# A first stage written out as a table of ten steps, in one stream of recurrences with the layers

## Chip, core and metric

One Trainium2 chip, one NeuronCore. A core has five engines with queues of their own: PE (TensorE, matmuls; PEld are its weight loads), DVE (VectorE), ACT (ScalarE), POOL (GpSimd) and SP (SyncE, which here issues DMAs). Each takes its instructions in the order of its queue. They meet through semaphores. SBUF holds tiles of 128 partitions; PSUM, eight banks of 128 x 512 float32, takes the results of PE. The metric is the device time of one launch in microseconds (us), lower is better.

## What is computed

Two blocks on x of 4 sequences (b) x 1024 tokens x 128 features, all float32. First a two-directional state-space block, whose result is added to x:

```python
xn = _layernorm(x, ln_w, ln_b)
y_fwd = _mamba(xn, ...)
y_bwd = flip(_mamba(flip(xn), ...))
return x + 0.5 * (y_fwd + y_bwd)

def _mamba(x, ...):
    xp, z = split(x @ W_in.T)                      # 256 channels each
    xc = silu(conv4(xp) + b_conv)                  # depthwise, 4 taps
    dt, Bm, Cm = split(xc @ W_x.T, [8, 24])        # 8, 16, 16
    dt = softplus(dt @ W_dt.T + b_dt)
    A = -exp(A_log)
    def step(h, inp):                              # 256 channels x 16 states
        h = h * exp(dt_t[:, :, None] * A) + (dt_t * u_t)[:, :, None] * B_t[:, None, :]
        return h, einsum('bdn,bn->bd', h, C_t)
    y = (scan(step) + xc * Dp) * silu(z)
    return y @ W_out.T
```

Then six layers of windowed attention (16 heads of 64, window 32, rotary embedding, normalised queries and keys) and a gated feed-forward block of 341. They need, besides the weights, a rotary table for each layer (multiplied by the layer's scales) and first weights and biases into which the layer norm's scale and shift are folded.

## The kernel before

There are two parts. **`mamba` (L153)** is the first stage. The order in which its instructions reach the queues is left to the framework's scheduler. `prepare(b, d, out)` does for sequence b and direction d all that comes ahead of the recurrence: load and normalise (for d = 0), transpose, convolution as four accumulated matmuls, gate product, Silu, the small projection `xdbl`, softplus as five ACT steps (L320 to L324) and three DVE steps (L328 to L330), and stores to DRAM: `gate`, `xcs` (convolved input), `bcd` (B and C) and `dts` (dt, and dt times the input). There are eight such (b, d) units. `scan(d, ready, m, more)` runs the recurrence of sequence 0 alone, for one direction and one half m of the channels, on tiles of 32 channels x 4 states by 1024 tokens: 4 x 16 such tiles, that is 128 tiles' worth of 512 tokens. Time runs along the free axis, one `tensor_tensor_scan` for each 512 tokens. Between the tiles it pulls pieces of the generator `beside()` (L483): the preparation of the other units, and for every layer `rotary` and `fold`. What is left of them follows after the last scan, then the projection of direction 1 and `store(0)`, which hands sequence 0 to the layers in `xsa`.

**`Layers` (L803)** is the rest, in a fixed order. Its 96 tiles (sequence, layer, 256 tokens) go through the table `ORDER`, one pass per tile; an entry `name-back` is the operation `name` for the tile that lies `back` passes behind. Entries of `ASIDE` (xd, xi, xr, xo, xt, xa, xy, xg, xp, xq) are turns of **`Beside` (L504)**, which runs the recurrences of sequences 1 to 3 beside the layers. It cuts them into units (b, d, half of time t, half of channels m) of 16 scan tiles of 8 channels x 16 states by 512 tokens, 384 in all, 6 in each pass of ORDER: `fetch`/`steps` loads `sdt0` and `sdt1` three tiles ahead (three buffers each, 256 KB a load), `decay` (L631) makes exp(dt A) on ACT into `da`, which has one PSUM buffer, `input` (L643 on POOL for odd tiles, L645 on DVE for even ones) makes the input term in `sh` (eight buffers), `scan` (L659) is on DVE, `output` (L672) multiplies by C on POOL, `add` (L692) sums over the states on PE for four tiles, `skip` (L705), `gate` (L716), and `piece` p or q advances the output projection. When the stream is over, the passes go on with `LAST_ORDER`, which has no turns of Beside. At the seam, the constants are made a second time (`make_consts`, L61, with the attention masks), SP issues the first layer's weights (24 DMAs), then `beside.start()` its first loads. In the first pass 8 x FIRST (L1353), one turn of each kind, runs eight tiles at once.

Of the kernel before, what the change touches and what calls it, by code (L numbers as in the profile page):

```python
# [18 lines left out]
P = 128  # L19
# [40 lines left out]
@with_exitstack  # L60
def make_consts(ctx, tc, pool, first):  # L61

    nc = tc.nc
    c = {}
    c["ident"] = pool.tile([P, P], F32, name="ident")
    make_identity(nc, c["ident"])
    if first:
        flip = c["flip"] = pool.tile([P, P], F32, name="flip")
        nc.gpsimd.memset(flip, 0.0)
        nc.gpsimd.affine_select(  # L70
            out=flip, in_=flip, pattern=[[1, P]], compare_op=ALU.not_equal,
            fill=1.0, base=-(P - 1), channel_multiplier=1,
        )

        ones = pool.tile([P, DG], F32, name="ones")
        nc.gpsimd.memset(ones, 1.0)
        nc.gpsimd.affine_select(
            out=ones, in_=ones, pattern=[[-SG, DG]], compare_op=ALU.is_ge,
            fill=0.0, base=0, channel_multiplier=1,
        )  # L80
        states = c["states"] = pool.tile([P, DG], F32, name="states")
        nc.gpsimd.affine_select(
            out=states, in_=ones, pattern=[[SG, DG]], compare_op=ALU.is_ge,
            fill=0.0, base=SG - 1, channel_multiplier=-1,
        )
    else:
        flip = c["flip"] = pool.tile([P, P], F32, name="flip")
        nc.gpsimd.memset(flip, 0.0)
        nc.gpsimd.affine_select(
            out=flip, in_=flip, pattern=[[1, P]], compare_op=ALU.not_equal,  # L90
            fill=1.0, base=-(P - 1), channel_multiplier=1,
        )

        wide = c["states"] = pool.tile([P, 2 * DG - DG8], F32, name="wide")
        nc.gpsimd.memset(wide, 0.0)
        nc.vector.tensor_reduce(
            wide[:, DG - DG8 : DG], c["ident"].rearrange("p (n i) -> p i n", i=DG8),
            AX.X, ALU.add,
        )
        ident16 = c["ident16"] = pool.tile([P, P], BF16, name="ident16")  # L100
        nc.vector.tensor_copy(ident16, c["ident"])
        mean = c["mean"] = pool.tile([P, P], F32, name="mean")
        nc.vector.memset(mean, 1.0 / D)
        center = c["center"] = pool.tile([P, P], F32, name="center")
        nc.vector.tensor_tensor(center, c["ident"], mean, ALU.subtract)

        tp = ctx.enter_context(tc.tile_pool(name="t_mask", bufs=1))
        m32 = tp.tile([P, 8, 2 * W], F32, name="m32")
        nc.gpsimd.memset(m32, 0.0)
        for r in range(4):  # L110
            q = m32[r * W : (r + 1) * W]
            nc.gpsimd.affine_select(
                out=q, in_=q, pattern=[[0, 8], [1, 2 * W]], compare_op=ALU.is_ge,
                fill=NEG, base=0, channel_multiplier=-1,
            )
            nc.gpsimd.affine_select(
                out=q, in_=q, pattern=[[0, 8], [-1, 2 * W]], compare_op=ALU.is_ge,
                fill=NEG, base=W, channel_multiplier=1,
            )
        mask = c["mask"] = pool.tile([P, 8, 2 * W], BF16, name="mask")  # L120
        nc.vector.tensor_copy(mask, m32)

        mask0 = c["mask0"] = pool.tile([P, 8, 2 * W], BF16, name="mask0")
        nc.vector.tensor_copy(mask0, m32)
        nc.vector.memset(
            mask0[0:W].rearrange("p (h x) j -> p h x j", x=2)[:, :, 0, 0:W], NEG
        )
    return c
# [23 lines left out]
@with_exitstack  # L152
def mamba(  # L153
    ctx, tc, dram, x, lnwb, win, wconv, wx, wdt, wout, vecs, alog, x1_dram, xsa, spilled,
    rope, qks, tabs, w1, lvec, w1f, lvf
):
# [3 lines left out]
    nc = tc.nc  # L160
    nc.scalar.preload_act_table_set("natural_log_exp_and_others")
    cp = ctx.enter_context(tc.tile_pool(name="m_const", bufs=1))
    c = make_consts(tc, cp, True)
    ident, flip, states = c["ident"], c["flip"], c["states"]
    eps = cp.tile([P, 1], F32, name="m_eps")
    nc.vector.memset(eps, EPS)

    x_tiled = x.rearrange("(n p) d -> p n d", p=P)
    lnwb_sb = cp.tile([P, 2], F32, name="lnwb_sb")
    nc.scalar.dma_start(out=lnwb_sb, in_=lnwb)  # L170
    w = []
    for d in range(2):
        wd = {

            "wtap": cp.tile([P, KC, DI], F32, name=f"wtap{d}"),
            "wz": cp.tile([P, DI], F32, name=f"wz{d}"),
            "wx": cp.tile([P, NC, NX], F32, name=f"wx{d}"),
            "wdt": cp.tile([RANK, DI], F32, name=f"wdt{d}"),
            "wout": cp.tile([P, NC, D], F32, name=f"wout{d}"),
            "vec": cp.tile([P, NC, 3], F32, name=f"vec{d}"),  # L180
            "nega": cp.tile([P, NC, NDG, NSG], F32, name=f"nega{d}"),
        }
        nc.scalar.dma_start(
            out=wd["wtap"], in_=wconv[d : d + 1].to_broadcast([P, KC, DI])
        )
        nc.scalar.dma_start(out=wd["wz"], in_=win[d, :, 0:DI])
        nc.vector.tensor_tensor(
            wd["wtap"], wd["wtap"], bc(wd["wz"], 1, [P, KC, DI]), ALU.mult
        )
        nc.scalar.dma_start(out=wd["wz"], in_=win[d, :, DI:])  # L190
        nc.scalar.dma_start(out=wd["vec"], in_=vecs[d].rearrange("(c p) k -> p c k", p=P))
        nc.scalar.dma_start(out=wd["wx"], in_=wx[d].rearrange("(c p) k -> p c k", p=P))
        nc.scalar.dma_start(out=wd["wdt"], in_=wdt[d])
        nc.scalar.dma_start(out=wd["wout"], in_=wout[d].rearrange("(c p) k -> p c k", p=P))
        na = wd["nega"].rearrange("p m q g -> p (m q g)")
        nc.scalar.dma_start(out=na, in_=alog[d])
        nc.scalar.activation(na, na, AF.Exp)
        nc.vector.tensor_scalar(na, na, -1.0, None, ALU.mult)
        w.append(wd)

    sp = ctx.enter_context(tc.tile_pool(name="m_seq", bufs=1))
    wp = ctx.enter_context(tc.tile_pool(name="m_work", bufs=2))
    ps = ctx.enter_context(tc.tile_pool(name="m_ps", bufs=4, space=PSUM))
    psd = ctx.enter_context(tc.tile_pool(name="m_psd", bufs=2, space=PSUM))
    psy = ctx.enter_context(tc.tile_pool(name="m_psy", bufs=1, space=PSUM))

    def one(name):

        return ps.tile([P, TC], F32, name=name, tag="bank")

    seq = [None] * B

    def load(b):

        x1 = sp.tile([P, NBLK, D], F32, name="x1b" if b else "x1")
        xl = sp.tile([P, NBLK, D], F32, name="xl")
        s = slice(b * NBLK, (b + 1) * NBLK)
        nc.sync.dma_start(out=x1, in_=x_tiled[:, s, :])
        mv, rstd = norm_stats(nc, sp, x1, NBLK, eps, "x")
        normalize(nc, xl, x1, mv, rstd, NBLK)  # L220
        mv, rstd = norm_stats(nc, sp, xl, NBLK, eps, "l")
        nc.gpsimd.tensor_tensor(x1, x1, xl, ALU.add)
        normalize(nc, xl, xl, mv, rstd, NBLK)
        if b:
            nc.sync.dma_start(out=x1_dram[:, s, :], in_=x1)
        seq[b] = (x1, xl)

    def prepare(b, d, out):

        if d == 0:  # L230
            load(b)
        yield
        xl = seq[b][1]
        wd = w[d]
        vec = wd["vec"]
        halves = [slice(t * TC, (t + 1) * TC) for t in range(NTC)]

        xnT = sp.tile([P, KC - 1 + T], F32, name="xnT")
        nc.gpsimd.memset(xnT[:, 0 : KC - 1], 0.0)
        for t in range(NTC):  # L240
            pm = one("pm")
            for i in range(4):
                k = t * 4 + i
                s = slice(i * P, (i + 1) * P)
                if d == 0:
                    nc.tensor.transpose(pm[:, s], xl[:, k, :], ident)
                else:
                    nc.tensor.matmul(
                        pm[:, s], lhsT=xl[:, NBLK - 1 - k, :], rhs=flip, start=True, stop=True
                    )  # L250
            at = KC - 1 + t * TC
            nc.vector.tensor_scalar(
                xnT[:, at : at + TC], pm, lnwb_sb[:, 0:1], lnwb_sb[:, 1:2], ALU.mult, ALU.add
            )
            yield
# [92 lines left out]
    def spread(name, src):  # L348
# [5 lines left out]
        )  # L354
        return tile_

    def scan(d, ready, m, more):


        wd = w[d]  # L360
# [1115 lines left out]
```

## Time and profile before

| what | value |
|---|---|
| runs | 4144.86 us median of 3 (4140.26 to 4152.97) |
| profiled execution, own time | 4133.05 us |
| its span, first to last instruction | 4131.3 us |
| mean granted TensorE clock | 0.952 |
| busy in the span | PE 3794.3, DVE 3385.5, POOL 3214.1, ACT 2952.0 us |
| DMA | 518.28 MB, 125 GB/s in the mean |
| Gelu of the layers' first and last tile | 747.1 and 4119.7 us |

The layers' first matmuls run at 584, and their second pass begins at 640. The stretch with ORDER lasts to about 2950, that with LAST_ORDER to the end. In lines of groups, "x" is the number of instructions, then busy us, mean ns of one, idle time of the engine just before them, and after "<-" who ended most of it. Matmul ends are modelled, so a busy PE isn't PE at its peak.

### The profile page before, as it was taken

What the parts mean: (1) busy time and instruction counts of PE and PEld (TensorE: products, weight loads), DVE (VectorE), ACT (ScalarE), POOL (GpSimd) and SP (SyncE); (2) the same over time, 40 slices, a digit from 0 to 9 for tenths busy, and PEclk for the clock granted to TensorE, in tenths of its full rate; (3) what the DMA queues carried; (4) which work ended last, traced back from release to release, by engine and by line L of the source; (5) the groups of instructions that cost most, each with busy time, mean ns of one, the idle gap of its engine ahead of it and who ended that gap; (6) DMA issues with size and microseconds to landing.
All of it is one profiled execution on the core that took longest, in us unless ns stands there. A gap on an engine that the chain in (4) does not pass through costs nothing.

```text
span 4131.3 us, 144710 instructions
## 1 busy us (share of the span) xinstructions
PE 3794.3 (92%) x62120; PEld 2433.6 (59%) x62120; DVE 3385.5 (82%) x5053; ACT 2952.0 (71%) x5533; POOL 3214.1 (78%) x2463
## 2 busy tenths in 40 slices
PE   5666757999999999999999999999999999999998
PEld 2122223666666666666666666666666666666666
DVE  4665637999999899999999999999777777777774
ACT  4654634787778777878777877778667777777776
POOL 3779519999989898999889999989666666666663
PEclk8766767999999999999999999999999999999999
DMA  5654244555555555555454555554212222222221
GB/s 191 204 174 161 108 152 138 152 161 153 153 144 149 146 153 155 154 151 164 139 149 144 157 157 164 161 143 132 65 56 60 60 64 62 60 60 61 58 60 43
DMA packets 308111, 518.28 MB, mean 125 GB/s; under 512 B 43464, under 2 KB 135120, under 8 KB 307472
## 3 DMA queue, kind: packets, MB, share of 16 engines
q1 hardware_dynamic: 303136, 506.74, 41.6%
q8 instruction: 491, 8.04, 0.8%
q10 hardware_dynamic: 4336, 2.28, 0.2%
q14 instruction: 148, 1.21, 0.1%
HBM read 362.85 MB, written 48.52 MB: 100 GB/s over the span
## 4 chain that ended last, share of the span: by engine, by line
PE 65%; ACT 8%; DVE 5%; POOL 4%; issue 2%; DMA 1%; SPq 0%; DVEq 0%; ACTq 0%; POOLq 0%
PE pq L905 13%; PE po L1090 10%; PE pw L1112 8%; PE pv L957 7%; PE pt L988 6%; PE sim L1027 5%; PE pe L1065 4%; PE py L1209 3%; PE pa L1193 3%; PE pg L1169 2%; ACT sq L912 2%; PE sim L1009 2%; PE acc L692 1%; DVE rot L925 1%; DVE r L925 1%
## 5 line engine op out<-in xcount | busy, mean ns | idle before, releaser
L938 POOL TENSOR_TENSOR r<-r,rot 128x512 f32<-128x512 f32 x768 | 965.0, 1275 | 81.0 <-DVE rot L925 70.5
L951 POOL TENSOR_TENSOR r<-r,n 128x1024 f32<-128x1024 f32 x384 | 726.7, 1907 | 252.8 <-ACT n L947 242.0
L905 PE MATMUL pq<-w,xsa 128*128 128x512 f32 x1536 | 798.0, 614 | 13.7 <-DMA w<-in_wqkv 11.4
L925 DVE TENSOR_TENSOR rot<-pq,tab 128x512 f32<-128x512 f32 x768 | 516.2, 683 | 139.5 <-ACT sq L912 107.7
L912 ACT ACTIVATE sq<-pq 128x512 f32<-128x512 f32 x768 | 448.4, 599 | 242.7 <-PE pq L905 124.8
L925 DVE TENSOR_TENSOR r<-pq,tab 128x512 f32<-128x512 f32 x768 | 518.2, 683 | 72.0 <-ACT sq L912 39.9
L1058 POOL TENSOR_TENSOR e<-e,sm 128x1024 f32<-128x1024 f32 x192 | 366.0, 1906 | 244.8 <-DVE sm L1054 231.5
L672 POOL TENSOR_TENSOR sh<-sh,sc 128x512 f32<-128x512 f32 x384 | 488.6, 1278 | 20.0 <-DVE sh L659 4.0
L988 PEld LDWEIGHTS pt<-ident,r 128*128 128x128 f32 x3072 | 358.3, 141 | 239.5 <-issue 111.7
L988 PE MATMUL pt<-ident,r 128*128 128x128 f32 x3072 | 443.1, 277 | 31.2 <-POOL r L951 17.2
L933 DVE TENSOR_REDUCE n<-sq 128x16 f32<-128x1024 f32 x384 | 456.4, 1209 | 0.0
L1090 PEld LDWEIGHTS po<-at,vs 64*64 64x64 f32 x12288 | 331.9, 135 | 191.2 <-issue 144.1
L1090 PE MATMUL po<-at,vs 64*64 64x32 f32 x12288 | 398.8, 222 | 11.4 <-ACT at L1071 7.8
L1090 PE MATMUL po<-at,v 64*64 64x32 f32 x12288 | 392.2, 220 | 12.0 <-issue 11.8
L957 PE MATMUL pv<-w,xsa 128*128 128x512 f32 x768 | 381.2, 598 | 0.0
L1112 PE MATMUL pw<-o,wos 128*128 128x256 f32 x1536 | 376.3, 388 | 0.8 <-issue 0.8
L631 ACT ACTIVATE da<-sdt,b_nega 128x512 f32<-128x512 f32 x384 | 264.6, 689 | 115.3 <-DVE sh L659 111.9
L1090 PEld LDWEIGHTS po<-at,v 64*64 64x64 f32 x12288 | 335.1, 136 | 12.6 <-issue 12.5
L1027 PEld LDWEIGHTS sim<-kT,qT 64*32 64x32 f32 x24576 | 264.1, 105 | 128.5 <-issue 121.8
L905 PEld LDWEIGHTS pq<-w,xsa 128*128 128x128 f32 x1536 | 255.8, 191 | 138.2 <-issue 58.4
L998 ACT COPY qT<-pt 128x512 f32<-128x512 f32 x384 | 229.0, 596 | 134.7 <-PE pt L988 134.7
L1037 DVE TENSOR_REDUCE mx<-sim 128x8 f32<-128x512 f32 x384 | 245.3, 681 | 93.4 <-PE sim L1027 93.3
(194 smaller groups left out, 7879.6 us busy)
## 6 DMA issues: line engine op xcount, KB each, us to landing
sdt<-dts SPq DMA_DIRECT2D x768, 256.0 KB
vs<-v SPq DMA_DIRECT2D x192, 384.0 KB
w<-in_wqkv SPq DMA_DIRECT2D x288, 128.0 KB
tab<-tabs SPq DMA_DIRECT2D x96, 256.0 KB
vs<-v SPq DMA_DIRECT2D x168, 128.0 KB
wos<-in_wo SPq DMA_DIRECT2D x96, 128.0 KB
gate<-pre SPq DMA_DIRECT2D x8, 1024.0 KB
dts<-e SPq DMA_DIRECT2D x32, 256.0 KB
```

Source lines behind the costliest of these rows:

```text
L672: self.nc.gpsimd.tensor_tensor(h, h, self.unit[k][2], ALU.mult)
L905: self.nc.tensor.matmul(pq, lhsT=self.tokens(t, i), rhs=w[:, g * 512 : (g + 1) * 512], start=True, stop=True)
L912: self.nc.scalar.activation(sq[:, g * 8 : g * 8 + 8], pq, AF.Square)
L925: self.nc.vector.tensor_tensor(out[:, g * 8 : g * 8 + 8], pq, tab, ALU.mult)
L933: self.nc.vector.tensor_reduce(n2[:, a, :], t.tiles["sq", (i, a)], AX.X, ALU.add)
L938: self.nc.gpsimd.tensor_tensor(r[:, :, to], r[:, :, to], rot[:, :, of], ALU.add)
L951: self.nc.gpsimd.tensor_tensor(r, r, bc(n2[:, a, :], 2, [P, H, DH]), ALU.mult)
L957: self.nc.tensor.matmul(pv, lhsT=self.tokens(t, i), rhs=w[:, g * 512 : (g + 1) * 512], start=True, stop=True)
L988: self.nc.tensor.transpose(pt[:, j * P : (j + 1) * P], rf[:, (g * 4 + j) * P : (g * 4 + j + 1) * P], self.c["ident"],)
L1027: self.nc.tensor.matmul(t.bank["s", g, par][r * W : (r + 1) * W, col : col + 64], lhsT=qT[rows, g * 4 + j, at : at + W], rhs=kT[rows, g * ...
L1090: self.nc.tensor.matmul(t.bank["w", g, x][64 * par : 64 * par + 64, j * P + r * W : j * P + (r + 1) * W], lhsT=v[rows, col : col + DH], rh ...
L1112: self.nc.tensor.matmul(t.bank["pw"], lhsT=wos[:, g * 4 + h, :], rhs=t.tiles["o", g][:, h, :], start=(g == 0 and h == 0), stop=(g == 1 and ...
```

## The change

`mamba` goes; a class `Prepare` takes its place, and everything, from the constants on, is in a fixed order.

- The recurrences of sequence 0 go into Beside's stream: its units start at b = 0, so it has 512 tiles of the 8 x 16 x 512 form. The old form of 32 x 4 x 1024 is gone.
- At first only the first half (512 tokens) of unit (0, 0) is prepared, its operations one after the other, with the normalisation of the other half between them. Then `beside.start()`, and ten steps by the table `FIRST_ORDER`: in each, 16 tiles of the stream, and operations of up to four of the seven other units (back 0 to 3), with the fold and the rotary table of one layer in six of them. What is left of unit (0, 0), the second direction's taps and decays, and the masks (`rest`) are put in at every fourth entry of the first step. After the ten steps, turns of Beside follow until sequence 0 has been handed over.
- The constants are made once. Weight loads, which ACT issued before, are issued by SP. Two evictions that DVE did go to ACT: `xn` (was L252) and `pe` (was L268). Prepare uses the five PSUM banks of the layers in place of four of its own, Beside its own three.
- `add` calls `skip` itself where the one before is still open; it returned before. `FIRST` goes.
- `Layers` takes constants, banks and the running Beside; ORDER and LAST_ORDER stay.

```diff
+class Prepare:
...
+    def xn(self, u, h):
+        at = KC - 1 + h * TC
+        self.nc.scalar.activation(
+            u.tiles["xnT", 0][:, at : at + TC], u.bank["tr", h], AF.Identity,
+            scale=self.lnwb[:, 0:1], bias=self.lnwb[:, 1:2],
+        )
...
+    def pe(self, u, m, h):
+        self.nc.scalar.activation(
+            self.pre(u)[:, m, h * TC : (h + 1) * TC], u.bank["cv", m, h], AF.Identity,
+            bias=self.beside.w[u.d][1][:, m, 0:1],
+        )
...
+    def run(self, late):
...
+        for f in load:
+            f(u, low)
+        self.mz(u)
+        self.tr(u, 0)
+        self.xn(u, 0)
+        self.taps(0)
+        beside.decays(0)
...
+        other = [partial(f, u, high) for f in load]
+        for i, f in enumerate(half(0)):
+            f()
+            if i < 2 * len(other) and i % 2 == 0:
+                other[i // 2]()
+        rest = [
+            partial(self.sv, u), partial(self.taps, 1), partial(beside.decays, 1),
+            partial(self.tr, u, 1),
+            partial(self.xn, u, 1), *half(1), *late,
+        ]
+        beside.start()
+        order = entries(FIRST_ORDER, NUMBERED)
+        n = len(units) - 1
+        for k in range(-FIRST_AHEAD, n + max(back for _, _, back in order) - FIRST_AHEAD):
+            for i, (name, args, back) in enumerate(order):
+                if name in ASIDE:
+                    beside.do(ASIDE[name])
+                elif 0 <= k + FIRST_AHEAD - back < n:
+                    getattr(self, name)(units[1 + k + FIRST_AHEAD - back], *args)
+                if rest and i % 4 == 0:
+                    rest.pop(0)()
+        while beside.streams < 1:
+            for name in ASIDE.values():
+                beside.do(name)
 class Beside:
...
-            for b in range(1, B) for d in range(2) for t in range(NTC) for m in range(NC)
+            for b in range(B) for d in range(2) for t in range(NTC) for m in range(NC)
...
-        if NDG * (g + 1) > self.at["output"] or (j == 0 and self.at["skip"] < k):
+        if NDG * (g + 1) > self.at["output"]:
             return
+        if j == 0 and self.at["skip"] < k:
+            self.skip()
...
+FIRST_ORDER = """
+wx0-2 dc11-3 sv-1 xp-0 sb-3 mz-1 r2-1 wx1-2 m2-1 ds01-3 xi-0 xi-0 xb0-2 xd-0 n2-1 xq-0 lr0-2
+xr-0 xd-0 xo-0 xb1-2 dt00-2 xr-0 ds11-3 tr0-1 xy-0 xi-0 xt-0 da00-2 dt01-2 xd-0 xi-0 db00-2 lf-1
+xr-0 fp-1 xt-0 xt-0 dd00-2 da01-2 xg-0 xn0-1 xo-0 xd-0 db01-2 xa-0 xp-0 xa-0 dc00-2 dt10-2 xa-0
+xr-0 xi-0 dc01-2 xd-0 da10-2 xo-0 dd01-2 xq-0 rm0-2 cv00-1 xy-0 xi-0 xr-0 xa-0 xt-0 rs0-2 ld-0
+xo-0 fv-1 xi-0 tr1-1 xt-0 xo-0 xd-0 xr-0 xg-0 xn1-1 db10-2 pe00-1 xa-0 xd-0 xt-0 cv01-1 ds00-2
+dc10-2 cz01-1 xr-0 dd10-2 xp-0 xt-0 xd-0 xi-0 pe01-1 cz10-1 lr1-2 xr-0 xo-0 xi-0 xt-0 xo-0 xq-0
+xd-0 xr-0 fa-1 pz01-1 xd-0 xi-0 cz00-1 pz10-1 cz11-1 xr-0 xt-0 xi-0 pz00-1 xo-0 xd-0 dt11-2 xo-0
+xo-0 xt-0 da11-2 xa-0 xt-0 xr-0 xi-0 xd-0 cv11-1 xo-0 xt-0 cv10-1 xp-0 pz11-1 s1-0 r1-0 xr-0
+m1-0 sg-2 xo-0 xi-0 xd-0 xr-0 n1-0 xq-0 xt-0 xd-0 pe11-1 pe10-1 xi-0 rm1-2 xo-0 xr-0 xi-0 xd-0
+ad-0 xr-0 xt-0 fs-1 s2-0 xa-0 db11-2 xo-0 dd11-2 ds10-2 si-1 xd-0 xi-0 xo-0 xr-0 xo-0 xt-0 rs1-2
+xt-0
+"""
+FIRST_AHEAD = 1
...
-FIRST = "input decay scan output fetch add skip gate"
```

The names in the table: `cv`, `cz`, `wx`, `dt` are matmuls (convolution, gate product, small projection, dt), `tr` the transposes; `xn`, `pe`, `pz` their evictions; `si` the Silu pair; `da`, `dc` softplus on ACT, `db`, `dd` on DVE; `s`, `r`, `m`, `n` with 1 or 2 the two normalisations; `sg`, `sb`, `ds`, `sv` stores; `ld`, `lf`, `lr` loads; `fp`, `fv`, `fa`, `fs` the fold and `rm`, `rs` the rotary table.

## Prediction

> **What bounds the kernel now.** I cut the span into stages with the view of busy time by stretch, since the change touches one stage. Columns: busy us with instruction counts for PE, PEld, DVE, ACT, POOL, then granted clock, DMA share, GB/s.
>
> ```profile
> 0.00:82.00 82.00, 39.45 (x85) 17.23 (x86) 31.70 (x86) 33.54 (x63) 20.60 (x23) 0.85 0.57 189
> 82.00:500.00 418.00, 290.84 (x737) 100.06 (x736) 257.88 (x364) 233.95 (x364) 322.84 (x145) 0.73 0.48 164
> 500.00:580.00 80.00, 50.78 (x142) 24.37 (x139) 35.96 (x74) 42.80 (x73) 8.96 (x15) 0.72 0.28 106
> 580.00:640.00 60.00, 22.82 (x29) 3.54 (x30) 21.21 (x24) 10.27 (x15) 26.11 (x33) 0.59 0.75 219
> 640.00:2880.00 2240.00, 2168.49 (x38413) 1439.66 (x38414) 2109.82 (x3061) 1730.23 (x3295) 2064.14 (x1701) 0.99 0.53 151
> 2950.00:4050.00 1100.00, 1084.94 (x20236) 752.26 (x20240) 837.09 (x1297) 801.60 (x1545) 699.91 (x497) 1.00 0.21 60
> ```
>
> Row one is preparation before the first scan (it starts at 81.9). Row two, scans beside preparation: no engine is full, POOL leads with 77%. Row three: preparation left over after the last scan, POOL at 11%. Row four: the layers' start. From 640 PE is busy 97 to 99%: there only less work counts, not less waiting. So the first 640 us hold the slack.
>
> The POOL timeline and the waits of 500 to 640 say what happens at the seam:
>
> ```profile
> 500.02 2.35 POOL L399 TENSOR_TENSOR xc<-xc,szl 128x1024 f32<-128x1024 f32 x1 [3.10 <-DVE xc L398]
> 572.42 0.20 POOL masks.py:197 MEMSET ident<- 128x128 f32 x1 [70.06 <-PE pm L434]
> 603.80 1.26 POOL L643 TENSOR_TENSOR sh<-sdt,sb 128x512 f32<-128x512 f32 x1 [24.27 <-DMA sdt<-dts]
> ```
>
> ```profile
> POOL sh L643 <- DMA sdt<-dts: 28.0, 3, 24.3
> ACT pb L598 <- DMA sb<-bcd: 20.2, 1, 20.2
> ```
>
> For 100 us no recurrence runs: one stream has ended, and the next waits for its loads behind the layers' weights.
>
> Prices of a 512-wide scan tile, from the groups by shape, 640 to 2880:
>
> ```profile
> L672 POOL TENSOR_TENSOR sh<-sh,sc 128x512 f32<-128x512 f32 x367 | 467.0, 1278 | 18.9 <-DVE sh L659 4.0
> L631 ACT ACTIVATE da<-sdt,b_nega 128x512 f32<-128x512 f32 x367 | 252.9, 689 | 83.7 <-DVE sh L659 83.6
> L659 DVE TENSOR_TENSOR_SCAN sh<-da,carry,sh 128x512 f32<-128x512 f32 x189 | 241.4, 1277 | 6.0 <-ACT da L631 3.7 <-issue 0.2
> L643 POOL TENSOR_TENSOR sh<-sdt,sb 128x512 f32<-128x512 f32 x185 | 236.3, 1277 | 17.4 <-DMA sdt<-dts 16.5 <-PE pq L905 0.8
> L659 DVE TENSOR_TENSOR_SCAN sh<-da,sh 128x512 f32<-128x512 f32 x179 | 217.5, 1215 | 7.7 <-ACT da L631 3.1 <-POOL sh L643 2.9
> L645 DVE TENSOR_TENSOR sh<-sdt,pb 128x512 f32<-128x512 f32 x184 | 123.6, 672 | 3.7 <-ACT pb L598 1.8 <-DMA sdt<-dts 1.8
> ```
>
> And what full DMA engines move:
>
> ```profile
> 60.00:63.00 3.00, 2.07 (x2) 0.49 (x2) 1.68 (x3) 0.59 (x1) 0.00 (x0) 0.50 1.01 396
> 598.00:602.00 4.00, 0.00 (x0) 0.00 (x0) 0.07 (x1) 0.69 (x1) 0.00 (x0) 0.50 1.07 292
> 602.00:606.00 4.00, 0.00 (x0) 0.00 (x0) 2.52 (x4) 0.69 (x1) 2.12 (x3) 0.50 0.93 258
> ```
>
> Rows of 4 KB reach 396 GB/s; the sdt loads (2 KB rows) 258/0.93 to 292/1.07, about 275, and 248/0.88 just before: I take 283.
>
> **The part before the scans.** Removed: preparing the whole first unit. Now half of it is prepared, normalisation not behind weight work. By the timeline's durations: x lands 5, two half normalisations to 14, transposes and xnT 16, two convolution groups (3.43 each) and two gate products 25, gate copies, half Silu and its table loads (1.28 each) 31, x_dbl 33, two rounds of the five ACT steps (3.2), three DVE steps (2.1) and copies 48, stores, loads and first scan 55. Bounds 48 to 65; all DMAs now queue on SP, and here they have room.
>
> **A full step.** Each holds 16 tiles, one preparation unit, one layer's folds and rotary tables.
>
> DMA: 32 sdt loads of 262 KB, 8.39 MB at 283, are 29.6 us; y, gate and half of b and c, 0.79 MB, 2.8. Preparation: gate and xcs stores 2.1 MB at 396, 5.3; dts stores 2.1 MB at 283, 7.4; x and x1 1.3 (every second unit); x_dbl 0.4; fold 1.8; tables 5.3. Sum 53.9. Before, the first stage's scans loaded 64 pieces of 524 KB, 33.6 MB in 4 KB rows (a piece served four groups of states); now the sdt loads of 160 tiles are 84 MB.
>
> ACT: 16 decays 11.0; five steps of softplus (L320 to L324, 3.19) four times 12.8; copies L333 2.3; Silu (1.91 twice) and two table loads 6.4; gate copies 2.3; six evictions moved here from DVE (L252, L268), at 0.65 between the copy's 0.586 and L320's 0.685, 3.9; normalisations 16 x 0.482 every second unit, 3.9; rest 1.7. Sum 44. DVE: 16 scans 19.9, 8 inputs 5.4, L328 to L330 and L334 11.0, statistics 3.5, rest 3: 43. POOL: 16 outputs 20.4, 8 inputs 10.2, carries and gate 2.8, tables (2.35 twice) 4.7, add 1.2: 39. PE: at granted clock 1 a 512-column pass is 0.43 (two "pq" passes 0.86); cv 32 passes, cz, wx, dt 8 each, 24; transposes, folds, projection 5; the sums over states 4.2 when four tiles' products run together, as at 707 (8 records in 1.06), 13.8 if one by one: 33 to 43.
>
> One coupling costs more than these sums: "da" has one PSUM buffer, so decay n+1 waits for scan n (83.6 us in the row of L631). Walking FIRST_ORDER, each scan starts after DVE's other work or after ACT's other work plus 0.69, whichever is later; with 0.15 for handovers the sixteen take 50.6, or 52.2 with statistics. So a full step is bound by DMA, 54, with this chain just under it.
>
> The ten steps by their largest bound: 46 and 45 (chain; step 0 also carries unit 0's second half, the second taps and the masks), 51 (chain), four full ones 215.6, 50.8 (no fold), 45.5, 36.5 (preparation runs out): 490.
>
> What no row shows is how closely ten such steps follow their bound. From below: in the layers PE is busy 2168 of 2240, 3% over: 506. From above: in the hand-fed turns of 606 to 640 DMA was busy 66%, 50% over; that order has no lookahead, so I bound at 20%: 588. I take 7%, 525: nearer the layers, since this is the same stream in a written-out order, but with three tiles' loads (10 us) as the only cushion against a store queued ahead of them on SP, where a waiting store holds every later load. If that cover goes, a 2 MB pair of stores costs up to 5 us a step.
>
> **The rule against it.** The Trainium skill, DMA: Bandwidth & Descriptors, section Where 436 GB/s comes from, gives about 358 GB/s as what HBM feeds one core. By it the sdt bill is 23.4, a full step falls to the chain's 51 to 52, and the stage loses some 15 us. The saturated rows say 283 for these loads, so I keep that. TensorE: Matmul & The Clock Gate, Part 1, says that an idle array falls back to half clock. By it, PE's 33 to 43 become 66 to 86 a step, far over 54; the rows say 0.73 here, 45 to 59. I take the rows: a PE that falls behind has fewer gaps.
>
> **The seam and the layers.** The weights' 24 issues now come behind the last step while three tiles are in hand: SP took 11 us for them, so until the layers' step 0, 20 (16 to 30). Its counterpart before begins at 640 (PE "pq" at 639.7). After: 55 + 525 + 20 = 600, so 40 earlier. Six tiles go to each step of ORDER. Before, 14 of 384 were done at 640; after, 166 of 512: 346 instead of 370 are left, four steps. Gelus are 36.68 apart in ORDER (747.1 to 2948.1, 60 steps) and 33.9 in LAST_ORDER: 11 us less. Masks and constants leave the seam, where POOL's 572 to 580 held the weights up; that lies in the 40.
>
> Total: the profiled execution's own time 4133.05 (span 4131.3 and 1.75 around it) minus 51 is 4082. The median of the runs is 11.8 above it; I leave that difference: 4144.86 - 51 = **4094**.
>
> **Rivals.** (1) The steps follow their bound like the layers do: 506 + 52 + 18 = 576, 64 + 11 less: 4070. For it: the order is written out; against: DMA at 0.95 for 200 us is nowhere in this trace. (2) The new feed gives it back: stretch 15%, 564, 55 and 21: 640, only the 11 remain: 4134, within the noise. For it: 2.5 times the scan loads, and ACT takes DVE's evictions. (3) Slower: ACT's queue waits for cold convolutions. The evictions now stand in ACT's order ahead of decays; at 0.54, as in 250 to 350, PE's 33 to 43 are 61 to 80; with 67 in the six heavy steps, 1.07 x (46+45+402+45+37) = 615, 55 and 20: 690, 50 later, less 11: 4184. It decides from about 61 us a step. For it: that stretch; against: its PE waited for POOL, now in smaller pieces. (4) It doesn't do what it says: batch 0's last projection isn't through after ten steps, and single-file turns of 3 us follow; five cost 15. That lies in the range.
>
> **Chances.** Forecast 0.46, (1) 0.22, (2) 0.12, (3) 0.20. Faster by over 0.3% (about what a measurement of this kernel can tell from no change) is the first and (1), 0.68. The range runs from 4050 (below it the steps beat their bounds) to 4180, short of (3)'s point, leaving out some 0.15.
>
> **What would show it.** First scan near 55; DMA share of 0.9 or more and about 270 GB/s in steps 3 to 6, 58 us apart; POOL without its 70 us gap; layers' first Gelu at about 707 instead of 747; ORDER's end about four steps sooner in the layers' count. Wrong if sdt waits are small while ACT waits on PE "cv", or if steps exceed 61.

## The result and the profile after

The kernel after takes 4167.8 us (median of 5 runs, 4157.4 to 4169.5), before 4144.9: a ratio of 1.0047, 95% interval 1.0029 to 1.0064. It is slower by half a per cent, where 4094 was forecast. The profiled execution has a span of 4155.7 us, 24.4 more than before, and that difference is followed here. (Of the experiments, one execution of e4, 4840.6 us at a granted clock of 0.735, fell into a slower state and is left out of its ratio.) Each of the layers' 96 tiles has one Gelu, so the Gelus mark the passes. The difference divides into three stretches:

| From the span's start, us | before | after | forecast change | measured change |
|---|---|---|---|---|
| to the layers' first Gelu | 747.1 | 759.2 | -40 | +12.1 |
| first Gelu to the 66th | 2395.3 | 2404.4 | -11 | +9.1 |
| the rest | 988.9 | 992.1 | 0 | +3.2 |

The first stretch has three parts, each longer than forecast: first scan at 57.2 (55), ten steps in 567 (525), and 28 (20) from there to the layers' second pass, which begins at 652 (before at 640). From the first scan's start, and then from the end of every 16th scan to the end of the next 16th, the ten steps took 57.9, 46.7, 59.9, 63.9, 63.4, 62.8, 62.3, 59.4, 47.8 and 43.2 us.

First the view of busy time by stretch of the kernel after: steps 0 and 1, three full steps, the last two, the seam, and the stretch with ORDER. Columns are those of the prediction.

```profile
57.00:114.00 57.00, 34.69 (x60) 8.74 (x59) 31.73 (x38) 23.94 (x35) 36.06 (x46) 0.68 0.63 198
114.00:160.00 46.00, 31.11 (x96) 12.70 (x97) 30.75 (x62) 26.98 (x41) 37.20 (x44) 0.80 0.82 235
220.00:284.00 64.00, 41.46 (x117) 16.02 (x116) 42.96 (x80) 40.19 (x65) 39.49 (x31) 0.76 0.91 271
284.00:348.00 64.00, 42.41 (x129) 16.74 (x127) 38.12 (x51) 41.71 (x68) 37.17 (x44) 0.78 0.88 270
348.00:411.00 63.00, 39.92 (x114) 15.69 (x115) 42.53 (x81) 40.68 (x66) 41.86 (x46) 0.76 0.92 277
532.00:580.00 48.00, 28.86 (x70) 8.26 (x68) 36.80 (x44) 25.40 (x42) 33.43 (x40) 0.70 0.92 301
580.00:623.00 43.00, 22.01 (x32) 2.40 (x32) 28.17 (x35) 13.64 (x23) 33.38 (x42) 0.66 0.87 253
623.00:652.00 29.00, 13.35 (x40) 5.07 (x40) 13.73 (x18) 5.32 (x8) 14.65 (x15) 0.73 0.94 272
759.00:2913.00 2154.00, 2091.62 (x37258) 1396.36 (x37241) 1993.92 (x2911) 1650.96 (x3159) 1918.75 (x1573) 1.00 0.50 144
```

In a full step no engine is busy for more than 43 of 64 us, near the sums forecast for each (PE 33 to 43, ACT 44, DVE 43, POOL 39). DMA is at about 0.9. That is the resource named, but a tenth short of full. A step holds 17.3 MB (270 GB/s for 64 us). In the ORDER stretch PE is busy 2092 of 2154, as before.

The waits of the full steps, kernel after, 220 to 470 (total us, times, longest):

```profile
POOL sh L671 <- DMA sdt<-dts: 73.6, 20, 12.0
PE pm L414 <- DMA w1s<-in_w: 57.3, 4, 15.7
...
PEld pm L414 <- DMA w1s<-in_w: 31.8, 2, 16.6
```

POOL waits for the tiles' loads, as it should if DMA binds. The two L414 lines are new: PE stands up to 15.7 us, and its weight load up to 16.6, at the first matmul of a layer's fold (`fp`), which needs weights that SP has only just asked for. They are one standstill seen twice: before the fold at 239.7, PE is idle for 13.58 us and PEld for 14.38 of the same time. The view of the tile `pm` on PE, 220 to 480, says who waits for PE's work on that tile, which is the fold, convolution and dt together:

```profile
who waited for it (us, times):
  ACT e L370: 18.8, 4
  ACT xnT L279: 10.8, 4
  POOL sh L671: 7.1, 4
```

The seam, kernel after, by SP's timeline and then POOL's:

```profile
616.69 9.78 SPq L634 DMA_DIRECT2D sdt<-dts  x8
626.52 6.46 SPq L884 DMA_DIRECT2D w<-in_wqkv  x12
633.02 1.97 SPq L884 DMA_DIRECT2D wos<-in_wo  x4
635.03 0.94 SPq L884 DMA_DIRECT2D w1s<-w1f  x2
636.02 1.28 SPq L884 DMA_DIRECT2D w2s<-in_w  x3
637.34 0.33 SPq L884 DMA_DIRECT2D lv<-lvf  x1
637.72 0.90 SPq L917 DMA_DIRECT2D tab<-tabs  x2
638.66 0.43 SPq L777 DMA_DIRECT2D sx<-x_dram  x1
639.19 2.45 SPq L634 DMA_DIRECT2D sdt<-dts  x4
```

```profile
632.97 1.27 POOL L700 TENSOR_TENSOR sh<-sh,sc 128x512 f32<-128x512 f32 x1 [0.17 <-DVE sh L687]
...
646.68 1.26 POOL L671 TENSOR_TENSOR sh<-sdt,sb 128x512 f32<-128x512 f32 x1 [12.45 <-DMA sdt<-dts]
```

SP needs 12 us to issue the 24 loads of weights and tables. Until then no further `sdt` load can start, and POOL's next tile comes 12.45 us late. DVE is held by the same issues: its step of the stream's next projection needs `sx`, whose load SP issues at 638.66, behind them, and the next scan (644.14) stands behind that step in DVE's queue:

```profile
643.53 0.69 DVE L797 SCALAR_TENSOR_TENSOR sx<-po,sx 128x512 f32<-128x512 f32 x1 [8.59 <-DMA sx<-x_dram]
```

The gap of 70 us at 500 to 572 is gone, as intended.

### The profile page after: what moved, and what is told of

It reads as the page before. It is cut to its first block, busy times and chain, and to the rows that moved or that the text cites. A ratio compares the mean times of both kernels' runs of the same rounds, so it can differ in the third digit from the quotient of the medians.

```text
span 4155.7 us, 145436 instructions
## 1 busy us (share of the span) xinstructions
PE 3790.7 (91%) x62120; PEld 2431.8 (59%) x62120; DVE 3407.6 (82%) x5073; ACT 2977.0 (72%) x5585; POOL 3163.0 (76%) x2589
## 4 chain that ended last, share of the span: by engine, by line
PE 66%; ACT 9%; DVE 9%; DMA 6%; POOL 5%; issue 4%; SPq 1%; DVEq 0%; POOLq 0%; ACTq 0%
PE pq L930 13%; PE po L1115 9%; PE pw L1137 7%; PE pv L982 6%; PE pt L1013 6%; PE sim L1052 6%; PE pe L1090 4%; PE pa L1218 3%; PE pg L1194 2%; DMA sdt<-dts 2%; PE py L1234 2%; DVE sh L687 2%; PE acc L722 2%; PE sim L1034 2%; POOL sh L700 1%
## 5 line engine op out<-in xcount | busy, mean ns | idle before, releaser
L700 POOL TENSOR_TENSOR sh<-sh,sc 128x512 f32<-128x512 f32 x512 | 648.7, 1272 | 40.4 <-DVE sh L687 16.0
L671 POOL TENSOR_TENSOR sh<-sdt,sb 128x512 f32<-128x512 f32 x256 | 325.8, 1273 | 281.1 <-DMA sdt<-dts 243.7
L659 ACT ACTIVATE da<-sdt,b_nega 128x512 f32<-128x512 f32 x512 | 352.2, 688 | 254.5 <-DVE sh L687 202.7
L687 DVE TENSOR_TENSOR_SCAN sh<-da,sh 128x512 f32<-128x512 f32 x256 | 312.2, 1219 | 104.3 <-POOL sh L671 53.8
L687 DVE TENSOR_TENSOR_SCAN sh<-da,carry,sh 128x512 f32<-128x512 f32 x256 | 327.0, 1277 | 84.9 <-POOL sh L671 47.9
```

Of the source, the lines that this page charges most:

```text
L687: self.nc.vector.tensor_tensor_scan(h, self.da.pop(n), h, self.carry[:, at : at + 1] if t else 0.0, ALU.mult, ALU.add)
L700: self.nc.gpsimd.tensor_tensor(h, h, self.unit[k][2], ALU.mult)
```

## The experiments

The theories after the result were these: transfers bind the full steps (forecast), or a wait at the fold's matmuls does, or SP's queue with three tiles in hand does; the seam's extra time is the weights' issues, or the odd tile in front of them; and the layers lose because an odd number of tiles is done at their start, which swaps POOL's and DVE's inputs, or because the four passes saved are worth nothing. Ratios are to the kernel before, on the same chip. "After" stands for 1.0047. Where the ten steps or the Gelus are compared, each kernel has one profile.

**e6: more transfers, no more work.** Gates and xcs are stored a second time, to a place that nobody reads: 16.8 MB more.

```diff
             ...
+            again = self.dr.tile([NC, P, T], F32, name=f"again{n.start}{u.b}{u.d}{s.start}")
+            self.nc.sync.dma_start(
+                out=again.rearrange("m p t -> p m t")[:, :, s], in_=self.pre(u)[:, n, s]
+            )
```

> The changed kernel with each of the two stores of convolved input and gate issued a second time, to a DRAM tile that nobody reads: 2.1 MB more for each unit, 16.8 MB in all, no engine work but 16 issues on SP. Theory A (the heavy steps are bound by transfers): 16.8 MB at 300 to 400 GB/s and a share of 0.9 are 47 to 62 us; some of it falls into the first two steps, where DMA has room, so 35 to 55 us more than the changed kernel, about 4210. Theory B (engines waiting for each other, loads hidden): under 10 us more.

Measured: 4188.8, ratio 1.0109 (1.0091 to 1.0127). Steps 3 to 6 went from 62 to 64 us to 66 to 69, the first Gelu from 759 to 799. One full step of this kernel, by stretch:

```profile
230.00:299.00 69.00, 44.35 (x116) 17.35 (x116) 43.34 (x81) 41.59 (x68) 38.03 (x30) 0.71 0.89 281
```

The engines' busy times are near those of after; over steps 3 to 6, 2.1 MB more cost 5 us a step. Transfers do bind. The 40 us in the stage are within theory A's 35 to 55, but by the ratios the whole kernel lost only 0.6%, some 26 us. In the profiles ORDER was 7 us shorter than in after, for no reason found.

**e5: fewer transfers.** The rotary tables of the six layers are neither loaded, scaled nor stored; the layers read the unscaled table, so the scales of q and k are missing from its output.

```diff
     ...
-        if u.l is None:
-            return
+        return
         ...
-            in_=self.dram[1][t.l, :, 2 * t.sb : 2 * t.sb + 2, :],
+            in_=self.dram[1][:, 2 * t.sb : 2 * t.sb + 2, :],
```

> The changed kernel without the rotary tables' multiplication in the first stage: loads, products and stores of the tables are left out and the layers read the unscaled table, so the scales of queries and keys are missing from the result. This takes 12.6 MB of transfers out of the six heavy steps, and 4.7 us of POOL a step, which is not the busiest engine. Theory A (DMA-bound): 2.1 MB a step at about 300 GB/s and a share of 0.9 are 7 to 8 us, so 40 to 46 us off the stage, time near 4125. Theory B (coupled engines): at most 10 off.

Measured: 4112.8, ratio 0.9923 (0.9907 to 0.9939). Full steps took 55 to 58 us, and the stage ended at 581 instead of 625. Two full steps:

```profile
210.00:266.00 56.00, 40.36 (x118) 15.86 (x117) 42.41 (x79) 41.22 (x67) 33.00 (x28) 0.77 0.87 261
266.00:322.00 56.00, 42.23 (x125) 17.18 (x124) 38.05 (x50) 40.34 (x66) 33.20 (x41) 0.77 0.88 269
```

The rate stays and the time falls with the bytes. This edit also spares POOL 4 to 6 us a step and SP its waits for POOL's products (26 us in the stage), so alone it wouldn't settle the point; with e6 it does.

**e3: the fold's matmuls later.** `fp` stood two entries behind its own load `lf`. It moves three rows down, and `fv` and `fa` follow it.

```diff
-xr-0 fp-1 xt-0 xt-0 dd00-2 da01-2 xg-0 xn0-1 xo-0 xd-0 db01-2 xa-0 xp-0 xa-0 dc00-2 dt10-2 xa-0
+xr-0 xt-0 xt-0 dd00-2 da01-2 xg-0 xn0-1 xo-0 xd-0 db01-2 xa-0 xp-0 xa-0 dc00-2 dt10-2 xa-0
...
-dc10-2 cz01-1 xr-0 dd10-2 xp-0 xt-0 xd-0 xi-0 pe01-1 cz10-1 lr1-2 xr-0 xo-0 xi-0 xt-0 xo-0 xq-0
+dc10-2 cz01-1 fp-1 xr-0 dd10-2 xp-0 xt-0 xd-0 xi-0 pe01-1 cz10-1 lr1-2 xr-0 xo-0 xi-0 xt-0 xo-0 xq-0
...
```

> The changed kernel with the fold's matmuls, vector and scalar steps moved later in the table, so that PE no longer stands at them until the weights loaded just before have landed (123 us of waits in the first stage, up to 17 each). Theory A (the stage is bound by what the DMA engines move, at 0.9): the heavy steps stay at 62 to 64 us, time within 8 us of the changed kernel. Theory B (PE's standstill holds convolutions, sums and so ACT's and POOL's queues): heavy steps fall by some 10 us each, time about 50 lower.

Measured: 4145.2, ratio 1.0001 (0.9991 to 1.0011). The steps: 58.1, 44.8, 56.4, 59.4, 61.5, 62.1, 61.6, 57.8, 47.7, 42.5; the ten steps end at 609, 15 earlier, and the first Gelu comes at 745. The waits of 220 to 470 and two full steps:

```profile
POOL sh L671 <- DMA sdt<-dts: 79.5, 22, 11.9
PEld pm L289 <- issue: 52.5, 110, 3.6
DVE sh L687 <- POOL sh L671: 47.4, 18, 6.6
```

```profile
275.00:334.00 59.00, 39.16 (x121) 15.29 (x120) 37.23 (x49) 37.73 (x63) 36.63 (x42) 0.84 0.92 281
334.00:394.00 60.00, 40.57 (x115) 14.54 (x113) 38.17 (x67) 38.63 (x65) 39.47 (x44) 0.84 0.91 276
```

The L414 lines are gone: nowhere in the stage does PE still wait for a fold's load. So the standstill was real: in the stage of after it is 79.0 us of PE in six folds. (The 123 of the expectation add 43.8 on PEld, which is the same time once more.) Most of it lay beside the transfers; some 16 us came out, where theory A had at most 8 and theory B 50. POOL's wait for loads stays.

**e4 and e10: six tiles in hand.** The first 144 tiles' `sdt` loads start six tiles ahead, in six buffers.

```diff
         ...
-            dt = self.dt[x][n] = self.sp.tile([P, TC], F32, name=f"sdt{x}", bufs=3)
+            pool, name, bufs = self.deep if self.deep and n < 144 else (self.sp, "sdt", 3)
+            dt = self.dt[x][n] = pool.tile([P, TC], F32, name=f"{name}{x}", bufs=bufs)
         ...
-        if n is not None and n + 3 < self.n:
-            self.steps(n + 3)
+        if n is None:
+            return
+        ahead = 6 if self.deep and n < 138 else 3
+        ...
```

> The changed kernel with the sdt loads of the first stage six tiles ahead in six buffers each instead of three (back to three for the last step). Bytes are the same. Theory A1 (DMA-bound, and what is lost between 0.9 and 1 is lost because three tiles are too short a cushion): DMA share of the heavy steps goes to 0.95 or more, steps 58 to 60, time some 25 lower. Theory A2 (0.9 is what mixed traffic gives): within 8 us. Theory B (engines wait for each other, not for loads): within 8 us, with POOL's sdt waits turned into others.

> The changed kernel with sdt loads six tiles ahead, for a profile at the usual granted clock (the median of its fast runs lay some 15 below the changed kernel). A1: heavy steps at 60 or less and DMA share of 0.95; A2: 62 to 64 as with three ahead, and the gain, if real, in the steps before and after.

Measured: 4152.6, ratio 1.0016 (1.0005 to 1.0027). That is some 13 below after by the two ratios, between the theories. e10 is the same kernel (4155.7 us), and its profile is the one read here. Its steps: 56.5, 49.1, 59.6, 64.3, 63.0, 65.0, 64.3, 50.6, 43.5, 41.9. The four full ones (3 to 6) gained nothing; the gain is in steps 7 and 8, which have no fold. Step 7 by stretch, then the waits of e10, 220 to 410:

```profile
479.20:529.70 50.50, 39.72 (x110) 13.97 (x109) 39.40 (x54) 38.72 (x61) 35.68 (x28) 0.83 0.99 306
```

```profile
PE pm L414 <- DMA w1s<-in_w: 46.9, 3, 16.8
ACT e L370 <- PE pm L359: 39.5, 3, 14.3
DVE sh L680 <- PE acc L729: 35.6, 3, 13.0
```

POOL's wait for `sdt` is no longer among the first, and PE's standstill at the fold has come through to ACT and DVE. In step 7 there is no fold to wait for, and the deeper cushion brings DMA to 0.99. In the full steps the fold's wait alone, with six tiles in hand, still holds the step at 63 to 65 us; the short cushion alone, with the fold out of the way (e3), at 59 to 62.

**e1: no odd tile.** After the ten steps, 160 tiles are done but sequence 0 isn't handed over; the closing loop, going round once for that, begins tile 161. Here the loop makes only the closing calls.

```diff
-            for name in ASIDE.values():
+            for name in ("add", "skip", "gate", "piece p", "piece q"):
```

> The changed kernel without the one extra tile after the ten steps: the layers start at tile 160 instead of 161, with each unit's turns one place later in the passes. Exchanging the two engines gave 7 us at most, so theory A (which engine takes which turn) has fallen; theory B (where units, projections and transfers meet the passes) expects first Gelu to Gelu 58 between 2096 and 2116, different from 2115 by some us either way; theory C (the trace before was lucky, run-to-run) expects 2112 to 2116 again. Time 4150 to 4170.

Measured: 4146.4, ratio 1.0009 (1.0000 to 1.0019). The first Gelu comes at 745.9, 13 earlier. POOL at the seam:

```profile
639.12 1.26 POOL L671 TENSOR_TENSOR sh<-sdt,sb 128x512 f32<-128x512 f32 x1 [8.93 <-DMA sdt<-dts]
```

The wait behind the weights' issues is still there, and from the end of the ten steps to the layers' second pass it takes 27.8 us, with the odd tile 27.7. So the odd tile costs nothing at the seam. Of the 13 us, 4 lie in the ten steps, whose instructions are those of after, and 10 in the layers' passes up to the first Gelu; e2 says why.

**e2: the two engines' shares swapped.** With an odd start, the tile whose input POOL forms falls on another place of ORDER. Here the parity is turned back for the layers.

```diff
+        beside.other = 1
...
-        if q % 2:
+        if (q + self.other) % 2:
```

> The changed kernel, but from the layers' first pass on the two engines that make the input term change places (DVE takes odd tiles, POOL even ones). The one turn after the ten steps leaves the stream at tile 161, an odd number, so in ORDER each input turn falls to the other engine than before. Theory A (odd start): the 22 us that the ORDER stretch loses between the first Gelu and the 59th come back; first Gelu still near 759, POOL's waits for sdt in that stretch near 17 us instead of 52, time about 22 below the changed kernel, about 4146. Theory B (the loss comes from another alignment of units and transfers with the passes): no change, 4160 to 4170.

Measured: 4160.5, ratio 1.0042 (1.0027 to 1.0056). One line of the waits from 759 to 2878, of after and of e2:

```profile
POOL sh L671 <- DMA sdt<-dts: 52.3, 38, 2.6
```

```profile
POOL sh L672 <- DMA sdt<-dts: 12.0, 10, 3.5
```

Forty us of waits went and nothing came of it there: first Gelu to the 66th took 2407.7 instead of 2404.4. In this stretch the theory of the odd start fell. PE is full there, and POOL's idle time is free. Ahead of it the theory holds, as the profiles show:

| run | ten steps' end to the second pass, us | second pass to first Gelu, us |
|---|---|---|
| after, e3, e5, e6, e10: odd start | 27.0 to 28.4 | 106.6 to 109.0 |
| e1: even start | 27.8 | 97.2 |
| e2: odd start, engines swapped | 30.3 | 97.2 |

From the second pass to the first Gelu, of after and of e2:

```profile
652.30:759.20 106.90, 78.91 (x1149) 47.37 (x1152) 95.20 (x127) 62.13 (x119) 99.96 (x77) 0.84 0.42 128
```

```profile
660.30:757.50 97.20, 77.01 (x1149) 44.94 (x1152) 92.55 (x125) 60.75 (x119) 96.87 (x75) 0.88 0.45 137
```

Here POOL is the fullest engine (94 and 99.7%), so it matters which inputs fall to it. Why that makes 10 us, when POOL's work differs by 3, wasn't tried. In the time of e2 the gain doesn't show: its profile has 6 us more in the ten steps, whose instructions are those of after, 3 at the seam and 3 in ORDER. Whether that is chance is open.

**e7: stop at 136 tiles.** The scan turns are left out of the ten steps once 136 tiles are done (128 of sequence 0, and 8 ahead); the layers do the other 24. The closing loop is that of e1.

```diff
-                if name in ASIDE:
+                if beside.at.get(ASIDE.get(name), 0) >= 136 and name in ("xi", "xd", "xr", "xo", "xt"):
+                    pass
+                elif name in ASIDE:
...
-            for name in ASIDE.values():
+            for name in ("add", "skip", "gate", "piece p", "piece q"):
```

> The changed kernel with the scan turns of the first stage stopped after 136 tiles, so that the ten steps end without the last 24 of their 160 tiles and without the odd one after them; at the layers' first full pass the stream stands where it stood in the kernel before, relative to sequence 1. Theory A (DMA-bound, and the last one and a half steps do work that ORDER would take at nearly no cost): 24 tiles at 2.7 us leave the stage, 50 to 65 us; four passes of ORDER come back at about 2 each, 8; and ORDER from first Gelu to Gelu 58 goes back from 2112-2116 to about 2096, if its loss was one of alignment. Together about 4100 to 4115. Theory B (preparation's own chain, back 3, sets the stage's end): within 15 us of the changed kernel.

Measured: 4101.5, ratio 0.9904 (0.9888 to 0.9919). The first Gelu comes at 704.5, 55 before after's and 41 before that of e1, which has the same closing loop. ORDER runs four passes longer, 63 instead of 59, and the time from the first Gelu to the 66th is 2400.9 against e1's 2404.0. So 24 tiles cost 41 us (1.7 each) ahead of the first Gelu and nothing behind it.

**e8 and e9: together.** e8 is e7 with e3's order; e9 is e8 with six tiles in hand for the first 128 tiles. Their diffs are those above, with 128 and 122 for 144 and 138 in e9.

> Both edits: scan turns stopped after 136 tiles, and the fold's steps later in the table. If the two gains are independent (22 measured for the fold, 50 to 70 for the tail) about 4085; if both fill the same gaps, like the short tail alone. Either way it should beat the kernel before by 0.7% or more.

> The short tail and the late fold, with the sdt loads of the first 128 tiles six ahead in six buffers each. If the tenth of the DMA engines' time that stays free in the heavy steps is lost to the short cushion (A1), the share there goes from 0.90-0.93 to 0.95 or more, the heavy steps from 60 to 57, and the time from 4080 to about 4062. If 0.9 is what this mixture gives (A2), 4074 to 4086.

Measured: e8 4079.6, ratio 0.9851 (0.9837 to 0.9866), first Gelu at 686.1. e9 4055.0, ratio **0.9781** (0.9762 to 0.9800), first Gelu at 659.3, the fastest of all and faster than both kernels. The gains of the late fold and the short tail add (about 4085 was expected for that), and e9 goes below the 4062 of theory A1. The first eight steps of e9 take 56.8, 42.4, 50.6, 53.8, 61.5, 53.1, 60.9 and 51.3. The short tail doesn't reach into these steps, so all kernels can be compared there:

| fold's wait | tiles in hand | first eight steps, us |
|---|---|---|
| as in after | three | after 476, e1 474, e2 483, e7 475 |
| as in after | six | e10 472 |
| moved | three | e3 462, e8 459 |
| moved | six | e9 430 |

The four of the first row have the same instructions in these steps, so they show how far one profile may stand from another. The full steps of e9 (3 to 6), then its waits of 220 to 450:

```profile
205.90:259.70 53.80, 39.58 (x116) 15.23 (x116) 42.87 (x80) 41.41 (x68) 37.98 (x29) 0.84 0.99 292
259.70:321.20 61.50, 42.46 (x125) 16.41 (x124) 37.17 (x50) 40.25 (x64) 38.30 (x43) 0.81 0.98 301
321.20:374.40 53.20, 39.54 (x116) 14.76 (x115) 42.09 (x80) 41.50 (x69) 40.69 (x45) 0.84 0.99 305
374.40:435.20 60.80, 44.43 (x133) 17.09 (x132) 37.59 (x49) 40.74 (x65) 35.88 (x29) 0.80 0.99 303
```

```profile
PEld pm L289 <- issue: 46.4, 104, 5.6
ACT da L668 <- DVE sh L696: 38.7, 31, 7.0
DVE sh L696 <- ACT da L668: 33.4, 30, 3.7
...
DVE sh L682 <- DMA fdt<-dts: 25.0, 5, 8.7
```

(`fdt` is the name of `sdt` with six buffers.) DMA is at 0.98 to 0.99: with the fold's wait gone and six tiles in hand, the steps follow the transfers. By turns they move some 16 and 18.5 MB, so they take 53 and 61 us. POOL's long waits for loads are gone; DVE still has some, and decay and scan wait for each other. The cushion is worth 27 us at the first Gelu here (e8 to e9).

## Why the prediction was wrong

**The step that failed: "I take 7%, 525."** The largest bounds were summed to 490, and ten steps were to exceed them by 7%. They exceeded them by 15.7%. Of the 42 us that this makes, 39 lie in the first eight steps: 476 where 1.07 times their bounds (408) is 437. What failed was the stretch. It was interpolated between two rows, with the written-out order as the reason for the lower end; that order had two hindrances in it that could be read from the diff, and with both removed the eight steps take 430 (e9):

- *The fold.* The prediction counted its bytes and its PE time, and never asked what is late when `fp` stands two entries behind `lf`. PE takes its work in order, so convolutions, dt and the sums over states queue behind one matmul: 79 us of PE in six folds, of which some 16 are time (e3, e8).
- *The cushion.* "With three tiles' loads (10 us) as the only cushion" was said, with up to 5 us a step as the price if it goes. It was gone in the full steps: POOL waits up to 12 us for a load there. From e8 to e9 it costs 28 us over the first eight steps, 3.5 a step. That is inside the price, but it stood outside the sum. While the fold's wait stands, the cushion alone gives 4 us of these steps (e10), no clear difference.

The bounds were a little low too: a full step moves some 17.2 MB and not 16.9, and at e9's 300 GB/s that is 57 us rather than 53.9. So in e9's full steps (229 us) the 7% on 216 would have come out by luck: it covers a bound that is 6% low, not waiting.

A check was at hand in the prediction's own text: "about 270 GB/s" and steps "58 us apart" make 15.7 MB, where its sum had 16.9. At 270 a step is 63 us, as measured. The sign named for being wrong, steps above 61 us, came true in steps 3 to 6.

Step 0 took 57.9 where 49 was meant, in every kernel (55 to 58), at a DMA share of 0.63 in after. It also holds the second half of the first unit and the masks, whose ordering cost wasn't worked out. Which of its waits counts wasn't tried.

**Transfers bind: right.** e6 and e5 show it from both sides, and e9 reaches a share of 0.99. On the rule weighed: where the Trainium skill (DMA: Bandwidth & Descriptors, Where 436 GB/s comes from) has about 358 GB/s for one core, e9's full steps move 292 to 305 at that share. The prediction's row of 396 lies above the page's figure. The rows were the better guide.

**PE's clock: right.** The full steps were granted 0.75 to 0.78, not half, and PE was busy for 40 to 42 us, inside 33 to 43. Rival (3) came out near in total (4184 against 4168), but by luck: its steps of 67 us by a cold PE didn't come. PE did hold ACT up (18.8 us at `e`, 220 to 480), by waiting at the fold. Rival (2) had the size of the stretch right, 15%, with half of its reason: the feed of loads is part of what gives the gain back.

**The seam: 28 instead of 20, inside its range of 16 to 30.** The issues took 12 us, 11 were taken. What they hold up was not worked out: POOL's tile (12.45 us) and DVE's projection step (8.59). Which of the two sets the 28 wasn't tried. Of rival (4)'s single-file turns there is one, and at the seam it costs nothing (27.7 with it, 27.8 without, e1). What it does is to leave an odd start, 10 us in the layers' first passes (e1, e2); the kernel before took 107 there too, so this is no part of the miss.

**Four passes: counted rightly, worth nothing.** ORDER passes to LAST_ORDER at the 59th Gelu instead of the 63rd. But the time from first to 66th Gelu doesn't follow the count:

| passes of ORDER | first to 66th Gelu, us |
|---|---|
| 63 | before 2395.3; e7 2400.9; e8 2401.9; e9 2401.7 |
| 59 | after 2404.4; e1 2404.0; e3 2402.0; e5 2401.7; e6 2397.6; e2 2407.7; e10 2412.5 |

The prediction set ORDER's mean, 36.68, against LAST_ORDER's 33.9. That mean holds passes with the stream's own output projection and hand-over (PE's lines L782 and L825 of after), mostly 38 to 42, and those of sequences 1 to 3 stay in ORDER either way. The whole of ORDER takes 2333.8 in e7 and 2203.2 in after: four passes are 130.6, or 32.6 each, no more than those of LAST_ORDER. So the 11 us weren't there to be had.

The sum of the misses, in the profiled execution: stage 42, first scan 2, seam 8, ORDER 20 and end 3, together 75 of the 75 between -51 and +24. Open is part of the ORDER term: before's 2395 is below all the others but is a single profile, and e6 (2397.6) and e10 (2412.5) show how far one profile may stand from the next.

## What to carry to other kernels

A hand-written order isn't priced by its sums: for each instruction that needs a load, count the entries between the load and it, and ask what queues behind it on its engine. Where two hindrances hold the same step, taking away either alone shows little (here, over eight steps, 4 us for the cushion, 16 for the fold, and 46 for both), so try them together before calling one harmless. Put work where the binding resource isn't the one it uses: 24 tiles cost 41 us in a stage bound by transfers and nothing in one bound by PE. Price a change in the number of passes by the passes that go, not by the mean.

## What the runs showed of the hardware that was not expected

The rate at a DMA share near 1 differed with what was moved: 292 to 305 GB/s in the full steps of e9, 292/1.07 = 273 for `sdt` loads in 2 KB rows before, 396 in three us of the kernel before with transfers in 4 KB rows. The granted clock was higher where PE stood still less, with 41 to 43 us of PE busy in each full step: 0.75 to 0.78 in after, 0.78 to 0.84 in e3. And waits counted on POOL (52 us against 12 in e2) told nothing of time where PE was full.
